# Layer 0 of a four-layer attention kernel: TensorE and VectorE in source order, an earlier normalisation, a look-up in three steps

## The chip, the cores and the metric

The kernel runs on one core of a Trainium2 chip. The metric is the device time of one execution in microseconds (us). A core has five engines that run side by side and wait for each other through semaphores: TensorE (PE; PEld is its loading of weights), VectorE (DVE), ScalarE (ACT), GpSimd (POOL) and SyncE (SP), which here issues the DMAs. Matrix products land in PSUM, the accumulator memory, and have to be evicted from there by VectorE or ScalarE before the same buffer can be used again.

## The reference

The input is four images of 56 x 56 positions with 256 channels in float32. Four layers follow one another; each adds its result to its input, and each normalises its input first over groups of eight channels. Only layer 0 matters here. It is attention over a 7 x 7 neighbourhood with zero padding, with eight heads of 32 channels:

```python
q = x @ wq.T + bq ; k = x @ wk.T + bk ; v = x @ wv.T + bv      # x: normalised
k_unf, v_unf = _unfold(k), _unfold(v)                          # 49 shifted copies, zero padded
logits = jnp.einsum('ndhw,ndkhw->nkhw', q, k_unf) * scale
attn = jax.nn.softmax(logits, axis=1)                          # over the 49 places
out = jnp.einsum('nkhw,ndkhw->ndhw', attn, v_unf)
return out @ wo.T + bo                                         # added to the layer's input
```

Layer 3 is attention in shifted windows with a bias that is read from a table of 169 rows by index: `bias = rel_bias_table[rel_index]`. The kernel makes that bias, with the window masks, while layer 0 runs.

## The kernel before, in words

Layer 0 works on two grids. The projections run over **chunks** of 448 positions (8 image rows), seven to an image (`NCH`), 28 in all. The attention runs over **blocks** of seven image rows, eight to an image (`NB0`), 32 in all, and each block has four **units** (`NTC`), pieces of 16, 12, 12 and 16 columns. Units 0 and 3 are the edge units, 1 and 2 the inner ones.

A chunk has seven steps. `prepare(r)` normalises the chunk on VectorE (L939, two instructions of 128x448), copies a few leftover columns and issues the load of the chunk after the next. `project_rows(r)` gives six steps: `values(0)`, `values(1)` (products L971, eviction with bias on VectorE L975, then a store of the values to DRAM), `keys(0)`, `keys(1)` (L945, four evictions on ScalarE L1190) and `queries(0)`, `queries(1)` (L945, evictions on ScalarE L1199). All of them, the output projection, the statistics and the look-up draw their PSUM tile from `ps_m`, which has two buffers in this layer.

`attend_pairs` runs the units. For unit w it does `logits(w)`: 16 products of float32 into the two tiles `ps_s` (L1058), a mask add on VectorE (`e`, L1065) followed by an exponential on ScalarE (L1066) for one half, and an exponential (L1068) followed by a product with a mask on GpSimd (L1069) for the other. Then come two adds on GpSimd for the unit before (`b`, L1078), then `w["fill"]()`, a list of steps of other work, then `products` of the unit before (L1087, into `ps_o`), and then its `done`, called `finish`: on VectorE a sum for blocks and units at the image's border (L1234), a reciprocal (L1237 or L1232) and the product that writes `attn` (L1239). `gather`, the first act of a unit, fetches the values it needs from DRAM.

`project_out(r)` is the output projection of block r in two steps (L945 with `w_wo`): each adds the residual on VectorE (`xr`, L1263); the second also takes the next layer's statistics (`bn_stats`, L894) and stores. `first_look(i)` takes the statistics of the next image's chunks (L894 on `x`), which `load(i, looks, "xs")` has fetched before. When all parts of an image are there, `group_stats` puts three steps on a list: `channels`, `mean` (a small product L912 and three small VectorE instructions on `dv`, L915 to L917) and `scale` (a second small product L921, then L922 and a power on GpSimd, L923). `step_stats` runs one of them; `known(l, b)` runs all that are pending.

`table_steps` makes the bias table of layer 3: seven calls of `look_up(q0)` and four of `mask(ty)`. One look-up casts indices and compares them with row numbers on VectorE (L1940, L1943), multiplies the resulting one-hot matrix with the table (L1947), copies the result (L1950), transposes it on TensorE (L1953) and copies again (L1954).

`stream` deals these steps out to the blocks, and `spread` cuts the list of a block into four equal parts. In layer 0 no engine is fixed, so this list is not the order of execution: a planner orders the instructions of each engine by what it expects to be ready and may move a step past others. Layer 1 has TensorE and VectorE in source order, layer 2 none, layer 3 four engines.

Of the kernel before, what the change touches and what calls it, by code (L numbers as in the profile page):

```python
# [24 lines left out]
FP = mybir.dt.float32  # L25
# [6 lines left out]
NIMG = 4  # L32
S = 56
T = S * S
C = 256
P = 128
CC = C // P
HD = 32
NH = 8
SCALE = HD ** -0.5  # L40
NCH = 7
CH = T // NCH
# [5 lines left out]
WN = 49  # L48
# [11 lines left out]
TR = 7  # L60
NB0 = S // TR
BT = TR * S
COLS = (0, 16, 28, 40, 56)
NTC = 4
# [766 lines left out]
def direct_blocks(ctx: ExitStack, tc: tile.TileContext, d: dict, watch):  # L831
# [44 lines left out]
    def ps_m():  # L876
        return psum_tile("m", m_bufs)
# [226 lines left out]
        products(held)  # L1104
        held["done"]()

    def spread(units, steps):

        n = len(units)
        for i, w in enumerate(units):  # L1110
            mine = steps[i * len(steps) // n:(i + 1) * len(steps) // n]
            w["fill"] = lambda mine=mine: [f() for f in mine]
            yield w

    def lazily(make, i, n):

        made = []
        return [lambda k=k: (made or made.extend(make(i)), made[k]()) for k in range(n)]
# [7 lines left out]
    def layer0(early, big, pool, brief):  # L1126
        types, width = tile_types()
        xs, looks = {}, {}
# [6 lines left out]
        def first_look(r):  # L1135

            add_stats(0, *divmod(r, NCH), looks.pop(r))
# [22 lines left out]
        def prepare(r):  # L1160
            c = r % NCH
            xn = xns[r] = brief.tile([P, CC, CH + P // 2], FP, tag="xn", name="xn0")
            x = xs.pop(r)
            at = left(c, CH)
            for h in range(CC):
                normalise(xn[:, h, at:at + CH], x[:, h, :], known(0, r // NCH), h)
            if at:
                end = left(c - 1, CH) + CH
                nc.scalar.copy(xn[:, :, :at], ahead[0][:, :, end - at:end])
            ahead[:] = [xn]  # L1170
            if 3 < r + 2 < NIMG * NCH:
                load(r + 2)

        def project_rows(r):

            b, g = divmod(r, NCH)
            xn = xns.pop(r)
            at = left(g, CH)
            v = brief.tile([P, 4, C], FP, tag="v", name="v0", bufs=1)

            def values(a):
                value_tiles(v, a, g, CH, xn, wv, bv0, vd[b])

            def keys(m):
                pm = project(wk, m * P, lambda h: xn[:, h, at:at + CH], CH)
                rows = pm.rearrange("p (r c) -> p r c", c=S)
                for i in range(NTC):
                    c0, n = key_range(*COLS[i:i + 2])
                    dst = (kE if i in (0, NTC - 1) else kI)[:, m, i // 2, 8 * g:8 * (g + 1), :]
                    nc.scalar.activation(dst, rows[:, :, c0:c0 + n], AF.Identity, bias=bk0[:, m:m + 1])  # L1190

            def queries(m):
                pm = project(wq, m * P, lambda h: xn[:, h, at:at + CH], CH)
                y = 8 * g
                while y < 8 * (g + 1):
                    i, y1 = y // TR, min((y // TR + 1) * TR, 8 * (g + 1))
                    if (b, i) not in q:
                        q[b, i] = brief.tile([P, CC, BT], FP, tag="q", name="q0", bufs=6)
                    nc.scalar.activation(q[b, i][:, m, (y - TR * i) * S:(y1 - TR * i) * S],  # L1199
                                         pm[:, (y - 8 * g) * S:(y1 - 8 * g) * S],  # L1200
                                         AF.Identity, bias=qbias[:, 0, m:m + 1], scale=SCALE)
                    y = y1

            return [lambda f=f, m=m: f(m) for f in (values, keys, queries) for m in range(2)]

        def pair(r, t):

# [59 lines left out]
            return [lambda m=m: step(m) for m in range(CC)]  # L1267

        def stream():
            n = NIMG * NCH  # L1270
            rows = []
            for c in range(2, n):
                rows += lazily(project_rows, c, 6)
                rows.append(lambda c=c: prepare(c + 1) if c + 1 < n else None)
            look_at = {}
            for b in range(NIMG - 1):
                for i in range(NCH):
                    look_at.setdefault(NB0 * b + min(i // 2 + (b == 0), 3), []).append((b + 1) * NCH + i)
            gone = 0
            for r in range(NIMG * NB0):  # L1280
                b, g = divmod(r, NB0)
                to = min(len(rows), (7 * (7 * r + 12)) // 8)
                steps, gone = rows[gone:to], to
                steps += [lambda i=i: first_look(i) for i in sorted(looks)]
                steps.append(lambda r=r: [load(i, looks, "xs") for i in look_at.get(r + 1, [])])
                for i in range(3 if g > 3 or g == 0 else 0):
                    steps.insert(2 * i, step_stats)
                if r:
                    steps += table[:3]
                    if len(table) in (1, 2, 3):  # L1290
                        steps.append(tables.close)
                    del table[:3]
                    at = (len(steps) + 1) // 2
                    steps[at:at] = project_out(r - 1)
                attns[r] = pool.tile([P, CC, BT], FP, tag="attn", name="attn0")
                yield from spread([pair(r, t) for t in range(NTC)], steps)

        for r in range(3):
            prepare(r)
            if r == 0:  # L1300
                load(3)
            if r < 2:
                for step in project_rows(r):
                    step()
        check_sizes(pool)
        tables = ExitStack()
        both = [tables.enter_context(tc.tile_pool(name=f"t{n}", bufs=n, side="right", reuse_waits="tile")) for n in (1, 2)]
# [613 lines left out]
    def table_steps(big, pool):  # L1921


        NR, NQ = 169, 7
        idx = big.tile([P, WN, WN], I32, name="idx")
        nc.sync.dma_start(out=idx.rearrange("p a b -> p (a b)"), in_=d["relidx"].to_broadcast([P, WN * WN]))
        row = big.tile([P, 2], I32, name="row")
        nc.gpsimd.iota(row, pattern=[[P, 2]], base=0, channel_multiplier=1)
        rowf = big.tile([P, 2], FP, name="rowf")
        nc.vector.tensor_copy(rowf, row)  # L1930
        tab = big.tile([P, 2, NH], FP, name="tab")
        nc.sync.dma_start(out=tab[:, 0], in_=d["table"][:P])
        nc.sync.dma_start(out=tab[:NR - P, 1], in_=d["table"][P:])
        t3 = big.tile([98, 4, 98], FP, name="t3")
        nc.sync.dma_start(out=t3, in_=d["c_m3"])
        base = big.tile([98, NH, WN], FP, name="base")

        def look_up(q0):
            idxf = pool.tile([P, NQ, WN], FP, tag="idxf", name="idxf")
            nc.vector.tensor_copy(idxf, idx[:, q0:q0 + NQ, :])  # L1940
            hot = pool.tile([P, 2, NQ * WN], FP, tag="hot", name="hot")
            for a, n in ((0, P), (1, NR - P)):
                nc.vector.tensor_scalar(hot[:n, a, :], idxf[:n].rearrange("p q k -> p (q k)"),  # L1943
                                        rowf[:n, a:a + 1], None, ALU.is_equal)
            pb = ps_m()
            for a, n in ((0, P), (1, NR - P)):
                nc.tensor.matmul(pb[:NH, :NQ * WN], lhsT=tab[:n, a, :], rhs=hot[:n, a, :], start=(a == 0), stop=(a == 1))  # L1947
            tb = pool.tile([NH, NQ, 98], FP, tag="tb", name="tb")
            for w in range(2):
                nc.vector.tensor_copy(tb[:, :, w * WN:(w + 1) * WN], pb[:NH, :NQ * WN].rearrange("p (q k) -> p q k", k=WN))  # L1950
            pt = ps_m()
            for q in range(NQ):
                nc.tensor.transpose(pt[:98, q * NH:(q + 1) * NH], tb[:, q, :], ident[:NH, :NH])  # L1953
            nc.vector.tensor_copy(base[:, :, q0:q0 + NQ], pt[:98, :NQ * NH].rearrange("p (q h) -> p h q", h=NH))  # L1954

        def mask(ty):
            m = pool.tile([98, NH, 98], FP, tag="m3", name="m3")
            for w in range(2):
                sl = slice(w * WN, (w + 1) * WN)
                nc.vector.tensor_tensor(m[:, :, sl], base, t3[:, ty:ty + 1, sl].to_broadcast([98, NH, WN]), ALU.add)  # L1960
            mv = m.rearrange("p (q j) k -> p q j k", j=4)[:, :, 2:4]
            nc.scalar.activation(mv, mv, AF.Exp)
            for pair in [3] if ty % 2 else range(3):
                nc.sync.dma_start(out=m3d[:, ty // 2, :, pair, :], in_=m)

        return [lambda q=q: look_up(q) for q in range(0, WN, NQ)] + [lambda ty=ty: mask(ty) for ty in range(4)]

    def check_sizes(pool):

# [178 lines left out]
        return tc.tile_pool(name=f"d{l}" + ("e", "", "w", "l")[k], bufs=(2, 1, 2, 2)[k],  # L2148
                            side="right" if l % 2 else "left", reuse_waits="tile")

    run(0, lambda own: layer0(*own), None, range(4))
    with pool_of(2, 0) as early, ExitStack() as ends:
        late = ends.enter_context(pool_of(1, 3))
        held = {}
# [102 lines left out]
```

## Time and profile before

| | us |
|---|---|
| median of 3 runs | 3981.41 (3980.17 to 3990.82) |
| the profiled execution | 3979.57 |
| its span, first to last instruction | 3977.7 |
| TensorE busy in the span | 3816.3 |
| VectorE busy | 2367.7 |
| GpSimd busy | 1745.9 |
| ScalarE busy | 1378.9 |
| layer 0, first logits to last residual product | about 38 to 802 |

The times of single instructions come from the profiled execution. Its span is what the profile's views divide up; the execution took 1.9 us more than the span. Layer 0 is about the first fifth. A row of groups or of waits names the line, the engine, the tile written and the tiles read.

### The profile page before, as it was taken

Reading aid. Unit: us, or ns where it says so; the run is one execution under the profiler, and the core shown is the slowest. Engines: PE = TensorE matmul, PEld = TensorE weight load, DVE = VectorE, ACT = ScalarE, POOL = GpSimd, SP = SyncE. Lnnn points to the kernel's source line nnn. Section 1 sums busy time; section 2 is a strip of 40 time slices with the busy share of each in tenths; the row PEclk is TensorE's granted clock in tenths of the full one; section 3 lists DMA queues with packets and bytes.
Section 4 is the critical chain, followed back from the end, with each engine's and each line's share of the span. In section 5 each row is a group of like instructions: output and inputs, shape, how many; then the busy total and the mean of one; then the engine's idle time right before and its main releaser. Section 6 shows DMA issues by size and latency. Waiting matters only on the chain. (4 is left out here: it accounts for less than half of the span.)

```text
span 3977.7 us, 92350 instructions
## 1 busy us (share of the span) xinstructions
PE 3816.3 (96%) x38871; PEld 2712.4 (68%) x38871; DVE 2367.7 (60%) x4431; ACT 1378.9 (35%) x2927; POOL 1745.9 (44%) x1883
## 2 busy tenths in 40 slices
PE   6999999889999999999999999999999999899998
PEld 4566666567777677776777767776676676566665
DVE  6777777734345544445444553446788877666665
ACT  3454545422222222222222222222555555344443
POOL 2576767721123312233112331123777777555555
PEclk9899999989999999999999999999999999999999
DMA  7343333320000100001000000001344443444443
GB/s 265 100 137 121 117 114 110 98 104 1 24 19 24 40 5 16 20 25 35 6 24 15 25 24 10 10 10 55 113 125 128 127 119 108 154 122 129 131 126 97
DMA packets 268659, 301.84 MB, mean 76 GB/s; under 512 B 25926, under 2 KB 260584, under 8 KB 267752
## 3 DMA queue, kind: packets, MB, share of 16 engines
q1 hardware_dynamic: 267946, 295.76, 24.4%
q8 instruction: 308, 5.05, 0.6%
q14 instruction: 117, 0.96, 0.1%
q10 hardware_dynamic: 288, 0.08, 0.0%
HBM read 203.39 MB, written 92.37 MB: 74 GB/s over the span
## 5 line engine op out<-in xcount | busy, mean ns | idle before, releaser
L1441 DVE TENSOR_TENSOR acc<-acc,ps_v 128x257 f32<-128x257 f32 x1104 | 463.4, 423 | 718.8 <-PE ps_v L1519 690.7
L1519 PE MATMUL ps_v<-xw,e 128*128 128x257 f32 x2208 | 612.3, 382 | 1.2 <-DVE acc L1441 1.2
L1514 PE MATMUL ps_o<-xw,at 128*128 128x257 f32 x2208 | 609.1, 380 | 0.0
L1409 PE MATMUL ps_s<-xnT,xd 128*128 128x512 f32 (+3 forms) x1344 | 573.2, 549 | 3.9 <-DVE xnT L1387 3.9
L1519 PEld LDWEIGHTS ps_v<-xw,e 128*128 128x128 f32 x2208 | 413.4, 189 | 142.4 <-issue 82.3
L1503 ACT COPY at<-ps_t 128x512 f32<-128x512 f32 (+3 forms) x332 | 170.4, 513 | 969.8 <-PE ps_t L1500 969.4
L1078 POOL TENSOR_TENSOR b<-e 126x336 f32<-126x336 f32 (+5 forms) x512 | 499.6, 996 | 9.3 <-ACT e L1066 1.2
L1514 PEld LDWEIGHTS ps_o<-xw,at 128*128 128x128 f32 x2208 | 419.3, 190 | 59.9
L945 PE MATMUL ps_m<-xn,w_wqkv 128*128 128x392 f32 x1024 | 375.5, 500 | 3.6 <-DVE v L975 1.9
L1402 POOL TENSOR_SCALAR xd<-xnT,vec 128x128 f32<-128x128 f32 x192 | 116.8, 619 | 569.9 <-PE ps_s L1409 566.1
L1069 POOL TENSOR_TENSOR e<-e,m0t 126x672 f32<-126x672 f32 (+3 forms) x128 | 238.5, 1863 | 266.5 <-ACT e L1068 253.5
L1069 POOL TENSOR_TENSOR e<-e,bias 119x784 f32<-119x784 f32 (+5 forms) x128 | 244.0, 1906 | 182.5 <-ACT e L1068 181.2
L1409 PEld LDWEIGHTS ps_s<-xnT,xd 128*128 128x128 f32 x1344 | 226.1, 191 | 142.0 <-issue 126.7
L1412 ACT ACTIVATE e<-ps_s 128x512 f32<-128x512 f32 x336 | 185.3, 552 | 348.4 <-PE ps_s L1409 341.4
L990 ACT ACTIVATE no<-rs 128x168 f32<-128x168 f32 (+2 forms) x256 | 93.8, 367 | 592.8 <-DVE rs L1841 280.3
L1087 PEld LDWEIGHTS ps_o<-e,vp 124*32 124x32 f32 (+3 forms) x8192 | 179.0, 111 | 141.6 <-issue 90.5
L945 PEld LDWEIGHTS ps_m<-xn,w_wqkv 128*128 128x128 f32 x1024 | 187.4, 190 | 125.2 <-ACT pr L2097 17.4
L1087 PE MATMUL ps_o<-e,vp 124*32 124x112 f32 (+3 forms) x8192 | 242.7, 255 | 6.0 <-POOL e L1069 4.4
L1066 ACT ACTIVATE e<-e 126x672 f32<-126x672 f32 (+5 forms) x256 | 219.5, 857 | 21.3 <-DVE e L1065 8.4
L939 DVE TENSOR_SCALAR xn<-x,gst 128x28 f32<-128x28 f32 (+4 forms) x368 | 207.4, 616 | 32.3 <-PE ps_m L945 22.9
L1841 DVE RECIPROCAL rs<-ps_o 128x196 f32<-128x196 f32 (+2 forms) x128 | 176.1, 1375 | 84.8 <-PE ps_o L1087 84.3
L971 PE MATMUL ps_m<-w_wqkv,xn 128*128 128x256 f32 (+1 forms) x800 | 206.0, 396 | 9.4 <-DVE xr L1876 6.0
(196 smaller groups left out, 6206.2 us busy)
## 6 DMA issues: line engine op xcount, KB each, us to landing
x<-xr SPq DMA_DIRECT2D x64, 392.0 KB
x<-in_x SPq DMA_DIRECT2D x53, 448.0 KB
x<-x SPq DMA_DIRECT2D x60, 392.0 KB
xr<-x SPq DMA_DIRECT2D x60, 392.0 KB
vd<-v SPq DMA_DIRECT2D x72, 256.0 KB
xr<-in_x SPq DMA_DIRECT2D x32, 392.0 KB
xr<-x SPq DMA_DIRECT2D x28, 448.0 KB
x<-xr SPq DMA_DIRECT2D x28, 448.0 KB
```

The lines of the kernel that those rows point to most:

```text
L939: nc.vector.tensor_scalar(dst, src, gst[:, h, 0:1], gst[:, h, 1:2], ALU.subtract, ALU.mult)
L945: nc.tensor.matmul(pm[:, :n], lhsT=w[:, h, col:col + P], rhs=rhs(h), start=(h == 0), stop=(h == CC - 1))
L971: nc.tensor.matmul(pm[:k, j * C:(j + 1) * C], lhsT=xn[:, h, first:first + k], rhs=w[:, h, :], start=(h == 0), stop=(h == CC - 1))
L1066: nc.scalar.activation(ev, ev, AF.Exp)
L1069: nc.gpsimd.tensor_tensor(parts(ev), parts(ev), w["emask"], ALU.mult)
L1078: nc.gpsimd.tensor_tensor(w["b"][a][:nk, :, :2 * nq].rearrange("p h (i c) -> p h i c", i=2), ev[:, :, :, 0, :], ev[:, :, :, 1, :], ALU.add)
L1087: nc.tensor.matmul(w["o"](k, i)[j * HD:(j + 1) * HD], lhsT=ones[:nk, :HD] if k else v(j, u), rhs=w["b"][j // 2][:nk, j % 2, i * nq:(i + 1) ...
L1409: nc.tensor.matmul(s[:, :n], lhsT=xd[j][:, h, :], rhs=xnT[:, h, first * P:last * P], start=(h == 0), stop=(h == CC - 1))
L1412: nc.scalar.activation(e[:, :n], s[:, :n], AF.Exp, scale=5.0)
L1441: nc.vector.tensor_tensor(acc[:, i, :], acc[:, i, :], pv[:, :C + 1], ALU.add)
L1514: nc.tensor.matmul(out[j][:, :C + 1], lhsT=e[:, col(i)] if i == j else at[:, col(i)], rhs=xw[:, i, :], start=(i == j), stop=(i == NB - 1))
L1519: nc.tensor.matmul(pv[:, :C + 1], lhsT=e[:, col(i)], rhs=xw[:, j, :], start=True, stop=True)
```

## The change

Four things are changed, all in layer 0.

1. The last line of the diff fixes TensorE and VectorE to source order for the whole layer; ScalarE, GpSimd and SyncE are still ordered by the planner.
2. `stream` is rewritten in the form that layer 2 has: each unit gets its own list `work[u]`. Three chunks are projected before the first block instead of two, and `needed(r)` says how many chunk steps have to be done by the end of block r: an even share, or what the next block reads, if that is more. The steps of a chunk alternate: values 0, keys 0, values 1, queries 0, keys 1, queries 1. The two steps of the output projection stand last in units 2 and 3, statistics first in units 0, 2 and 3, a first look in units 0, 1 and 2.
3. `prepare(c + 1)` stands behind the second of the six projection steps of chunk c and no longer behind the sixth, that is, half a chunk ahead.
4. `look_up` is cut in three: `look_up` (cast and compare), `rows_of` (product with the table and copies), `turn` (transposes and copy). They stand in units 0, 1 and 2 of a block, so that a block holds one look-up.

```diff
-    def spread(units, steps):
-
-        n = len(units)
-        for i, w in enumerate(units):
-            mine = steps[i * len(steps) // n:(i + 1) * len(steps) // n]
-            w["fill"] = lambda mine=mine: [f() for f in mine]
-            yield w
...
-            return [lambda f=f, m=m: f(m) for f in (values, keys, queries) for m in range(2)]
+            return [lambda f=f, m=m: f(m) for f, m in ((values, 0), (keys, 0), (values, 1), (queries, 0), (keys, 1), (queries, 1))]
...
-            for c in range(2, n):
-                rows += lazily(project_rows, c, 6)
-                rows.append(lambda c=c: prepare(c + 1) if c + 1 < n else None)
+            for c in range(3, n):
+                steps = lazily(project_rows, c, 6)
+                steps.insert(2, lambda c=c: prepare(c + 1) if c + 1 < n else None)
+                rows += steps
...
+            def needed(r):
+
+                b, g = divmod(min(r + 1, nb - 1), NB0)
+                last = min(TR * (g + 1) + 3, S)
+                c = next(c for c in range(NCH) if c == NCH - 1 or (c + 1) * CH // P * P >= last * S)
+                return max(min(len(rows), len(rows) * (r + 1) // (nb - 1)), 7 * (b * NCH + c - 2))
+
             gone = 0
-            for r in range(NIMG * NB0):
+            for r in range(nb):
                 b, g = divmod(r, NB0)
-                to = min(len(rows), (7 * (7 * r + 12)) // 8)
-                steps, gone = rows[gone:to], to
-                steps += [lambda i=i: first_look(i) for i in sorted(looks)]
-                steps.append(lambda r=r: [load(i, looks, "xs") for i in look_at.get(r + 1, [])])
-                for i in range(3 if g > 3 or g == 0 else 0):
-                    steps.insert(2 * i, step_stats)
+                to = needed(r)
+                work = [rows[gone + (to - gone) * u // NTC:gone + (to - gone) * (u + 1) // NTC] for u in range(NTC)]
+                gone = to
+                for u, i in enumerate(sorted(looks)):
+                    work[u].append(lambda i=i: first_look(i))
+                work[3].append(lambda r=r: [load(i, looks, "xs") for i in look_at.get(r + 1, [])])
+                for u in (0, 2, 3) if g > 3 or g == 0 else ():
+                    work[u].insert(0, step_stats)
                 if r:
-                    steps += table[:3]
-                    if len(table) in (1, 2, 3):
-                        steps.append(tables.close)
-                    del table[:3]
-                    at = (len(steps) + 1) // 2
-                    steps[at:at] = project_out(r - 1)
+                    for u in range(3):
+                        if table:
+                            work[u].append(table.pop(0))
+                            if not table:
+                                work[u].append(tables.close)
+                    for u, step in zip((2, 3), project_out(r - 1)):
+                        work[u].append(step)
                 attns[r] = pool.tile([P, CC, BT], FP, tag="attn", name="attn0")
-                yield from spread([pair(r, t) for t in range(NTC)], steps)
+                for u in range(NTC):
+                    w = pair(r, u)
+                    w["fill"] = lambda steps=work[u]: [f() for f in steps]
+                    yield w
...
-            if r < 2:
-                for step in project_rows(r):
-                    step()
+            for step in project_rows(r):
+                step()
+        prepare(3)
...
+            held[q0] = hot
+
+        def rows_of(q0):
+            hot = held[q0]
             pb = ps_m()
...
+        def turn(q0):
+            tb = held.pop(q0)
             pt = ps_m()
...
-        return [lambda q=q: look_up(q) for q in range(0, WN, NQ)] + [lambda ty=ty: mask(ty) for ty in range(4)]
+        return [lambda f=f, q=q: f(q) for q in range(0, WN, NQ) for f in (look_up, rows_of, turn)] + [lambda ty=ty: mask(ty) for ty in range(4)]
...
-    run(0, lambda own: layer0(*own), None, range(4))
+    run(0, lambda own: layer0(*own), {E.PE, E.DVE}, range(4))
```

## The prediction

> **What bounds the kernel now.** I read the page first: the span, the row of busy time and the slices.
>
> ```profile
> span 3977.7 us, 92350 instructions
> ...
> PE 3816.3 (96%) x38871; PEld 2712.4 (68%) x38871; DVE 2367.7 (60%) x4431; ACT 1378.9 (35%) x2927; POOL 1745.9 (44%) x1883
> ...
> PE   6999999889999999999999999999999999899998
> DVE  6777777734345544445444553446788877666665
> ```
>
> TensorE is busy nearly everywhere, so only its idle time and its slow stretches can be won or lost. A slice is 99.4 us; layer 0 is the first eight, and there VectorE (DVE) stands at 7 tenths, not 4: the second engine is near its limit just where the change works. The changed program's instruction order, read engine by engine, differs from the old one only up to the end of layer 0; behind it the order is the same on all five. So I asked for the windows of the four images of layer 0 (the first from the first logits at 38 us, each cut where its block 7 stores its output) and for TensorE's waits in them. Columns: window and length, PE, PEld, DVE, ACT, POOL busy, granted clock, DMA share, GB/s.
>
> ```profile
> 38.00:258.20 220.20, 190.91 (x2742) 121.12 (x2741) 168.25 (x262) 91.72 (x214) 118.72 (x93) 0.91 0.53 156
> 258.20:439.50 181.30, 166.96 (x2846) 113.22 (x2844) 136.81 (x190) 91.17 (x216) 125.25 (x101) 0.99 0.38 115
> 439.50:620.70 181.20, 166.87 (x2845) 113.04 (x2844) 136.76 (x189) 91.13 (x216) 125.12 (x101) 0.99 0.38 116
> 620.70:802.00 181.30, 161.77 (x2958) 109.82 (x2956) 135.38 (x188) 86.31 (x198) 130.69 (x104) 0.94 0.33 102
> ```
>
> TensorE idles 29.3 us in the first, 14.3 in each middle one, 19.5 in the last: 77 us in all, plus what the low clock costs. The waits of the second image (what waited, for whom; us, times, longest):
>
> ```profile
> PE ps_m L945 <- DVE attn L1239: 4.5, 2, 3.6
> PE ps_s L1058 <- DVE e L1065: 2.9, 5, 0.9
> PE ps_m L945 <- DVE dv L922: 2.1, 1, 2.1
> PE ps_m L921 <- DVE dv L917: 1.8, 1, 1.8
> PE ps_m L971 <- DVE xr L1263: 1.5, 2, 1.0
> PE ps_m L945 <- ACT kE L1190: 1.0, 1, 1.0
> ```
>
> The last row matters most. It is one place, in the timeline: a unit whose filling is keys, queries, output projection, three products for two `ps_m` buffers.
>
> ```profile
> 334.03 1.12 PE L1058 MATMUL ps_s<-q,kI 32*126 32x84 f32 x32
> ...
> 336.56 0.85 DVE L1065 TENSOR_TENSOR e<-ps_s,m0t 126x672 f32<-126x672 f32 x1
> ...
> 337.44 0.76 ACT L1066 ACTIVATE e<-e 126x672 f32<-126x672 f32 x1
> ...
> 338.11 0.37 ACT L1190 ACTIVATE kE<-ps_m,vec 128x152 f32<-128x152 f32 x1
> ...
> 339.35 1.58 PE L945 MATMUL ps_m<-attn,w_wo 128*128 128x392 f32 x4 [0.99 <-ACT kE L1190]
> ```
>
> Mask add on DVE (after the previous finish), exponential on ACT, then the eviction of the keys, then the third product: it starts 5.3 us after the unit, 0.99 us late.
>
> [...] the key eviction above sat ready behind the exponential. [...] behind the 5.7 us wait at 60 us, four 448-column matmuls took 3.36 us instead of 1.67. [...] the normalise of 448 columns took 0.42 to 2.41 us, mean 1.03 in the second image, and the three `dv` ops of 128x2 up to 2 us each.
>
> **The change part by part.** The sum is made against the profiled execution: 3979.6 us, span 3977.7 plus 1.9 around it; the median shown, 3981.4, is 1.8 above it.
>
> *What goes.* (a) The output projection moves to units 2 and 3 of a block, the last `attn` of the block before is written in unit 0: the waits for attn vanish in images 0 to 2, 4.2 + 4.5 + 4.5 = 13. In the last image they sit in blocks without filling and at the drain, and stay. (b) The old order pulled the 42 bn_stats (0.61 us) of images 1 to 3, with their 21 loads, into the first 120 us, and ran up to three table look-ups in one unit. DVE was late with values (11.2 + 2.3 us of waits in image 0) and look-up copies (3.1): 16.6. The new order takes the statistics two or three tiles per block and one look-up per block. (c) Waits for `xr`, 0.9 + 1.5 + 1.5 = 4. (d) Clock: 0.91 over 191 busy us of image 0 is up to 17 us; I take 10, as short waits remain. Sum 44.
>
> *What comes.* The block of eight products (v, k, v, q, k, q and two o) is now v | k | v q o | k q o, where the old order mostly had two to a unit. (e) Third product after k and q: 15 units at the measured 1.0 = 15. (f) Third product after v and q: the v eviction queues on DVE behind the mask add, this behind the finish of an edge unit (0.39 + 1.55 + 0.39), this in unit 1 behind a pair of normalises (2.07 mean). From the start of the unit that is 3.6 + 0.9 + 0.7 = 5.2 us against 4.6 for the three groups ahead on PE (1.05 + 1.95 + 1.6); with bn_stats in the units before, up to 2 late. 10 units at 0.8 = 8. (g) Seven table blocks. Step one (cast 0.6, two compares 1.4) and two bn_stats (1.2) stand ahead of a finish, so the next mask add is some 2 us late and with it the evictions: four units q v T / v q T / k q T at about 1.9. With k t o and q t o the third product is up after 3.2 us and its buffer free at 5.3 and 5.0: three at 2.1, three at 1.8. Together 19. (h) Statistics: the early `prepare` of a new image calls `known`, which runs the pending steps at once: matmul, three `dv` ops, matmul, power on POOL, on an in-order PE. Three times; one chain is 1 us free and up to 4.5 with POOL in the way; the old order paid 3.9 as well, so I add 3 each. In blocks 20 and 28 the `dv` ops (3.5 to 4.1 in the trace) stand before a v eviction in a v q o unit: 2.5 each more. Together 14. (i) The even share against what the next block needs leaves blocks 18 and 22 nearly empty, 26 empty and 23 overfull: 6. Blocks 26, 30, 31 without filling replace the old 29 to 31, at 17.3 us a block either way: 0. Sum 62.
>
> *Costed at nothing.* Three chunks before the stream instead of two and a bit: the same matmuls, earlier. The x loads, v stores, gathers and residual loads keep their number on SP (one row more); xs has four slots, and a DMA share of 0.38 covers them; if a load came late, DVE would stand on its bn_stats with the mask add behind, about 2 us a time. `prepare` earlier: covered by the half chunk of matmuls (5 us). POOL keeps its order.
>
> Net: 62 - 44 = +18, so 3997.6 against the profile and 3999 against the median; I say **3998 us**.
>
> Bounds. Unseen are (f), (g), (h), (i) as such, each from neighbouring rows: 0 to 15, 9 to 28, 3 to 22, 1 to 10. A gain from any is excluded: each is a wait added. (e) lies between 8 (ACT free earlier) and 18. Savings: 30 to 55, by how much clock and bn_stats congestion really go. So the whole runs from 21 - 55 = -34 to 93 - 30 = +63; the ends together are unlikely.
>
> **Rivals.** *Main: two buffers, three products.* For it: the 0.99 us case, seen twice in the middle images. **R1, faster.** The waits at DVE and clock in images 0 to 2 are removed, and the ring is milder because each eviction is ready sooner than my serial count. For it: DVE is idle 44 us of 181 per image, and the first image is 39 us longer than the others. With savings 55 and costs 31 (e 12, g 9, h 6, rest 4): -24, 3957. It decides where a third product costs less than about 0.4 us on average. **R2, no change.** What VectorE loses in order it gains in evenness: costs 46, savings 44; 3983. **R3, much slower.** DVE becomes the bound of the first image: a block of mask adds 3.9, finishes 7.7, residuals 2.4, values 1.1, normalises 2.1, bn_stats 2.4, look-up 3.2 is 22.8 us of DVE against 22 to 23 of PE; at 27 us a block the seven table blocks cost 15 more: +35, 4016. **R4, it does not act**: excluded, the orders differ.
>
> **How the numbers follow.** About 0.3%, 12 us, is what a measurement can tell from no change. Main 0.42, of which 0.05 falls short of 12 us; R3 0.15; R2 0.13; R1 0.30. So slower 0.37 + 0.15 = 0.52, same 0.05 + 0.13 = 0.18, faster 0.30. The likeliest case alone spans 3990 to 4010. The range 3946 to 4030 takes in R1 and R3 with some 12 us on either side; beyond it I leave 1 to 2 in 10.
>
> **What would show it.** Right: waits of `ps_m` L945 for kE and q evictions rise from 1 us to about 5 us in the middle images, waits for attn fall to nothing there, bn_stats of x are spread over 500 us, image 0 is no shorter than before by over 10 us. Wrong: middle images under 181 us; a first image under 205; idle of TensorE in layer 0 under 70 us in all; the clock at 0.97 or more in the first 250 us.

## The result, and the profile after

The changed kernel takes 4025.09 us (median of 4 runs, 4020.46 to 4026.93) against 3981.80 for the kernel before, run beside it: 43 us slower, a ratio of 1.0104 with a 95% interval of 1.0092 to 1.0117. The direction is the one forecast and the time lies in the forecast's range, but the shift does not fit: +16 was forecast, +43 measured. The profiled execution took 4026.93 us with a span of 4025.1, 47.4 more than the span before.

The page of the changed kernel, the same rows as before:

```profile
span 4025.1 us, 92357 instructions
...
PE 3832.5 (95%) x38871; PEld 2716.4 (67%) x38871; DVE 2380.8 (59%) x4431; ACT 1377.3 (34%) x2927; POOL 1749.9 (43%) x1883
...
PE   7788989989999999999999999999999999899998
DVE  5778777753444544445434454445687877666665
```

TensorE issued the same 38,871 matmuls and was busy 16 us longer. VectorE's first eight slices are as full as before. The windows of the four images, cut at the same stores (the first logits now come at 48.85 us, since three chunks lie ahead of them instead of two; columns as before):

```profile
48.85:279.27 230.42, 191.83 (x2880) 122.61 (x2880) 168.37 (x228) 88.32 (x205) 124.90 (x97) 0.87 0.34 105
279.27:467.91 188.64, 166.89 (x2794) 111.14 (x2796) 146.72 (x211) 91.61 (x215) 129.63 (x102) 0.96 0.52 147
467.91:664.64 196.73, 173.76 (x2858) 115.28 (x2850) 142.99 (x206) 90.62 (x215) 125.53 (x100) 0.97 0.37 113
664.64:850.04 185.40, 163.79 (x2856) 109.40 (x2844) 132.03 (x185) 83.86 (x193) 123.67 (x98) 0.94 0.32 101
```

Layer 0 ends at 850.0 us instead of 801.5: 48.5 us later. All of the loss is here; what follows took 1.1 us less. The 48.5 us have two parts. Over the whole of layer 0, start included, TensorE's busy time rose from 708.6 to 727.2 us and its idle time from 92.9 to 122.8. So **29.9 us are more waiting and 18.6 us are the same products at a lower clock**: the first image fell from 0.91 to 0.87, the two middle ones from 0.99 to 0.96 and 0.97. The clock records of the two traces agree: in layer 0 the clock was halved for 68 us before and for 113 us after. (Image by image the lengths don't compare, as the new list moves products between images.)

The waits of TensorE in the second image, which answer to the six rows shown of before. The change moves some lines of the kernel: the evictions of keys (L1190 before) are now L1182, those of queries (L1199) L1191, the residual (L1263) L1255.

```profile
PE ps_s L1058 <- DVE e L1065: 9.4, 8, 1.6
PE ps_m L945 <- ACT q L1191: 3.4, 3, 2.5
PE ps_m L921 <- DVE dv L917: 3.3, 1, 3.3
PE ps_o L1087 <- POOL b L1078: 2.4, 4, 1.0
PE ps_m L945 <- ACT kE L1182: 1.6, 2, 1.0
PE ps_m L912 <- DVE mv L908: 1.2, 1, 1.2
```

The row of attn (4.5) is gone. The evictions of keys and queries cost 5.0 instead of 1.0, and the logits wait 9.4 us for the mask add where it was 2.9. In the first image the greatest rows are these:

```profile
PE ps_m L921 <- DVE dv L917: 8.3, 1, 8.3
PE ps_m L1960 <- ACT q L1191: 7.4, 2, 4.6
PE ps_m L1960 <- DVE v L975: 5.9, 1, 5.9
PE ps_s L1058 <- DVE e L1065: 4.5, 5, 1.1
PE ps_m L1960 <- ACT kE L1182: 4.4, 1, 4.4
```

L1960 is the product with the table, `rows_of` (L1947 before): 17.7 us of waiting in four places, not for its own operand but for a free `ps_m` buffer. Before, the look-up had one row in this image:

```profile
PE ps_m L1953 <- DVE tb L1950: 3.1, 4, 1.1
```

One of the four in the timeline, from the first unit of a block into its second (start, length, engine, line, operation):

```profile
125.08 2.28 DVE L939 TENSOR_SCALAR xn<-x,gst 128x448 f32<-128x448 f32 x1
125.86 1.99 PE L971 MATMUL ps_m<-w_wv,xn 128*128 128x256 f32 x8
...
127.29 1.14 DVE L894 BATCH_NORM_STATS2 st<-x 128x6 f32<-128x448 f32 x2
127.69 1.67 PE L945 MATMUL ps_m<-xn,w_wq 128*128 128x448 f32 x4
128.35 0.32 DVE L1949 CAST idxf<-idx 128x343 f32<-128x343 int32 x1
128.71 2.79 DVE L1952 TENSOR_SCALAR hot<-idxf,rowf 128x343 f32<-128x343 f32 x2
...
131.43 0.37 DVE L1226 TENSOR_TENSOR rs<-ps_o,outside 128x224 f32<-128x224 f32 x1
131.83 1.55 DVE L1229 RECIPROCAL rs<-rs 128x224 f32<-128x224 f32 x1
...
133.73 0.85 DVE L1065 TENSOR_TENSOR e<-ps_s,m0t 126x672 f32<-126x672 f32 x1
...
134.49 0.68 DVE L975 TENSOR_TENSOR v<-ps_m,bc 128x512 f32<-128x512 f32 x1
...
135.23 2.55 PE L1960 MATMUL ps_m<-hot,tab 128*8 128x343 f32 x4 [5.87 <-DVE v L975]
...
142.05 3.35 PE L945 MATMUL ps_m<-xn,w_wk 128*128 128x448 f32 x4
```

The filling of the first unit of this block is all VectorE's (normalise, bn_stats, cast, compares: 6.5 us in the lines shown) and has no product, so TensorE is through with it at once and already makes values and queries of the second unit while VectorE is still comparing. Finish, mask add and eviction of the values follow in source order; the third product waits 5.87 us for that eviction. Behind the wait the clock is half (from 131.97 to 145.63 us in the clock record): the table product takes 2.55 us (1.41 where nothing waited, below) and the keys still take 3.35 instead of 1.67, seven microseconds later.

### The profile page after: what moved, and what is told of

It is laid out like the page before. It is cut to its first block, busy times and chain, and to the rows that moved or that the text cites. A ratio compares the mean times of both kernels' runs of the same rounds, so it can differ in the third digit from the quotient of the medians.

```text
span 4025.1 us, 92357 instructions
## 1 busy us (share of the span) xinstructions
PE 3832.5 (95%) x38871; PEld 2716.4 (67%) x38871; DVE 2380.8 (59%) x4431; ACT 1377.3 (34%) x2927; POOL 1749.9 (43%) x1883
## 5 line engine op out<-in xcount | busy, mean ns | idle before, releaser
L945 PEld LDWEIGHTS ps_m<-xn,w_wqkv 128*128 128x128 f32 x1024 | 188.0, 190 | 127.1 <-ACT pr L2113 17.1
L939 DVE TENSOR_SCALAR xn<-x,gst 128x28 f32<-128x28 f32 (+4 forms) x368 | 211.9, 629 | 18.8 <-ACT q L1801 5.9
L1019 POOL TENSOR_TENSOR e<-e,m3l 98x784 f32<-98x784 f32 x64 | 118.3, 1848 | 217.7 <-ACT e L1016 217.7
```

The costliest lines, as they stand in the source:

```text
L939: nc.vector.tensor_scalar(dst, src, gst[:, h, 0:1], gst[:, h, 1:2], ALU.subtract, ALU.mult)
L945: nc.tensor.matmul(pm[:, :n], lhsT=w[:, h, col:col + P], rhs=rhs(h), start=(h == 0), stop=(h == CC - 1))
```

## The experiments

"New list" is the dealing of the changed kernel, "old list" that of the kernel before. Times are medians of four or more runs; each ratio is to the kernel before, run beside it on the same chip. The versions were timed on several chips, on which the kernel before had medians of 3980 to 3984 us, so a difference of some 5 us between two versions decides nothing.

**Order alone, list alone.** First the new list without the fixed engines:

```diff
-    run(0, lambda own: layer0(*own), {E.PE, E.DVE}, range(4))
+    run(0, lambda own: layer0(*own), None, range(4))
```

> The changed kernel with no engine fixed in layer 0: the new lists of units, the table in three steps, the early normalise, but the planner's order again. Theory A (the fixed source order costs: VectorE's table compares and statistics stand ahead of the finish and the mask add because nothing may pass them, TensorE then waits over 3 us and falls to half its clock): the planner moves them, no wait of 4 us for an eviction is left in the first image, clock there 0.91 or more, time 3970 to 3995. Theory B (the dealing costs: three products to a unit for two ps_m buffers, blocks overfull and empty, in whatever order): 4005 to 4025, with the same crowded blocks.

Measured 3958.08, ratio 0.9942 (0.9926 to 0.9959). Theory B fell, and theory A fell short of the gain: the new list by itself makes the kernel 23 to 25 us faster. The longest wait for an eviction that is left in the first image is 3.7 us. (In the first image of the changed kernel each of the four waits over 3 us, of 4.65, 5.87, 8.26 and 4.43 us, came with half clock, which lasted 6.8, 13.7, 17.1 and 10.2 us. That is no limit for other places: in the kernel before, a wait of 3.05 us at 44 us was followed by keys at 1.77 us, full speed.) Then the old list with the fixed engines, the same line changed the other way in the kernel before:

> The kernel before with TensorE and VectorE fixed to source order in layer 0 and nothing else changed. Theory A: slower than before by 20 us or more, since this list holds three whole look-ups in a unit and the statistics of the next image in the first 120 us, and nothing may pass them now. Theory B: the old list deals about two products to a unit, so the middle images keep 181 to 184 us and the whole stays within 10 us of before.

Measured 4023.82, ratio 1.0103 (1.0086 to 1.0120). Fixing the order costs 42 us on the old list and 67 on the new one. In the old list three whole look-ups stand in a unit, each with its product right behind its compares, and nothing passes them: the table product waits for its compares seven times, 22.8 us in all, three times for over 6 us. The first of these reads, in TensorE's timeline,

```profile
90.38 2.55 PE L1947 MATMUL ps_m<-hot,tab 128*8 128x343 f32 x4 [6.12 <-DVE hot L1943]
```

Theory A, +20 or more, held; theory B, that the old list would stay within 10 us, fell.

**Which engine's order.** The changed kernel with `{E.PE}` or `{E.DVE}` in place of both:

> The changed kernel with TensorE alone in source order in layer 0; the planner orders VectorE too. Theory A1 (VectorE's fixed order is the cost: casts, compares, bn_stats and the statistics chain stand in source order ahead of finish and mask add): 3955 to 3985, near the 3958 of the version with no engine fixed. Theory A2 (TensorE's fixed order is the cost: a product whose buffer or operand is late holds up the products of attention behind it): 4010 to 4025, near the changed kernel. Both together: in between.

Measured 3963.22, ratio 0.9940 (0.9923 to 0.9956).

> The changed kernel with VectorE alone in source order in layer 0; the planner orders TensorE. Theory A1: 4005 to 4025. Theory A2: 3955 to 3985, since TensorE can take the products of attention ahead of a table product or a third product that has to wait.

Measured 4014.36, ratio 1.0066 (1.0050 to 1.0083). Theory A1 held in both: VectorE's fixed order makes nearly all of the loss; fixing TensorE besides adds about 11 us, and fixing TensorE alone adds 5, which is not clear of noise. What VectorE's freedom does can be seen in the same block as above, now with TensorE alone fixed:

```profile
110.06 1.76 DVE L1952 TENSOR_SCALAR hot<-idxf,rowf 128x343 f32<-128x343 f32 x2
...
129.10 1.99 PE L971 MATMUL ps_m<-w_wv,xn 128*128 128x256 f32 x8
129.91 0.39 DVE L1231 TENSOR_TENSOR attn<-ps_o,rs 128x224 f32<-128x224 f32 x1
130.22 0.85 DVE L1065 TENSOR_TENSOR e<-ps_s,m0t 126x672 f32<-126x672 f32 x1
130.93 1.67 PE L945 MATMUL ps_m<-xn,w_wq 128*128 128x448 f32 x4
131.13 0.69 DVE L975 TENSOR_TENSOR v<-ps_m,bc 128x512 f32<-128x512 f32 x1
132.52 1.42 PE L1960 MATMUL ps_m<-hot,tab 128*8 128x343 f32 x4
...
134.83 0.68 DVE L1952 TENSOR_SCALAR hot<-idxf,rowf 128x343 f32<-128x343 f32 x2
```

Values, queries, table: three products in the same order, and no wait. The normalise and the compares of this look-up were done at 110 to 117 us, units earlier, and those of the next fill the gaps behind, so that finish, mask add and eviction of the values come without a break.

**The look-up out of the way.** The table steps run between the projection steps of chunks 1 and 2:

```diff
             for step in project_rows(r):
                 step()
+                if r:
+                    for f in table[:3]:
+                        f()
+                    del table[:3]
...
```

> The changed kernel with the whole look-up (seven look-ups, four masks) run between the projection steps of chunks 1 and 2, ahead of the first block; the blocks hold none. Theory C (the table blocks of the first image trip the clock: compares late by collisions with GpSimd, then mask add, eviction and third product late): waits at the table product (17.7 us) and its copies (4 us) vanish from the blocks, the clock of the first image goes from 0.87 to 0.95 or more, the start grows by 5 to 15 us, net 15 to 28 us faster than the changed kernel: 3997 to 4010. Theory B (the ring of two with three products to a unit, in all four images): 0 to 10 us faster, 4015 to 4025, and the first image still shows waits of 3 us and a clock under 0.92.

Measured 4001.00, ratio 1.0048 (1.0031 to 1.0064): 24 us faster than the changed kernel, as theory C had it, though by other parts than expected. The first logits came at 94 us, 45 later and not 5 to 15, with 15 us more idle time of TensorE and a clock of 0.76 there; the first image's blocks took 172.5 us at a clock of 0.98 instead of 230.4 at 0.87. (How long the compares take beside GpSimd can be read in the changed kernel: the two during which no GpSimd instruction ran took 0.38 and 0.40 us, the other twelve 1.15 to 2.12.) The third image kept its length, 198 us. With the planner's order the same edit brings nothing:

> No engine fixed in layer 0 and, besides, the whole look-up ahead of the first block. Theory C (the look-up in the blocks costs beside the order): the last wait at the table product (3.7 us) goes, the clock of the first image rises above 0.955, another 5 to 15 us below the 3958 of the version with no engine fixed: 3943 to 3953. Theory A alone (the planner already hides the look-up): no gain, 3955 to 3968, as the start grows by what the blocks save.

Measured 3962.08, ratio 0.9942 (0.9926 to 0.9959), no faster than 3958: theory A alone, the planner had already hidden the look-up.

Running only the casts and compares ahead of the first block would have separated VectorE's lateness from the third product at one stroke (written down beforehand: 12 to 22 us faster, or under 6). It has no time: with the seven one-hot matrices kept, 2.7 KB per partition are left in SBUF where the look-up's other tiles need 14.2. The edits below take the question in steps.

**Two products to a unit.** Both engines fixed, the table in its place, only the dealing changed: five projection steps to a block, cut 2, 1, 1, 1. The normalise keeps its place but is no longer a step of its own, so that a chunk counts six steps. `upto[r]` is the even share, raised ahead of time for what later blocks need.

```diff
-                steps.insert(2, lambda c=c: prepare(c + 1) if c + 1 < n else None)
+                if c + 1 < n:
+                    steps[2] = lambda c=c, f=steps[2]: (prepare(c + 1), f())
...
-                to = needed(r)
-                work = [rows[gone + (to - gone) * u // NTC:gone + (to - gone) * (u + 1) // NTC] for u in range(NTC)]
+                to = upto[r]
+                sizes = {4: (1, 1, 1, 1), 5: (2, 1, 1, 1), 6: (2, 2, 1, 1)}.get(to - gone, (1, 1, 1, 0))
+                work = [rows[gone + sum(sizes[:u]):gone + sum(sizes[:u + 1])] for u in range(NTC)]
```

> The changed kernel, both engines fixed, with the projection steps dealt 5 to a block (a few 4 or 6) and cut 2, 1, 1, 1 to the units, so that with the output projection no unit outside the table blocks has more than two products and no block between 0 and 25 is empty or overfull. Theory B (the third product for two buffers and the uneven dealing, costed at 15 + 8 + 6 us in the forecast, are real): images 1 and 2 fall from 189 and 197 us to 181 or less, 20 to 30 us faster than the changed kernel, 3995 to 4005. Theory A (order, the first image): images 1 and 2 gain under 5 us each, the whole stays at 4013 to 4025.

Measured 3950.40, ratio 0.9910 (0.9894 to 0.9927): 75 us faster than the changed kernel, far more than either theory gave; the middle images fell to 181.3 and 175.6, as theory B had it. Counted in the lists, the changed kernel has 43 of 128 units with three or more products and 62 with one or none; this one has 7 and 33. Its windows:

```profile
48.85:250.19 201.34, 176.69 (x2884) 114.79 (x2884) 162.30 (x229) 88.06 (x205) 125.14 (x98) 0.97 0.39 120
250.19:431.50 181.31, 166.33 (x2803) 113.42 (x2804) 149.13 (x211) 92.19 (x218) 126.34 (x99) 0.95 0.54 154
431.50:607.05 175.55, 164.91 (x2859) 113.51 (x2851) 142.69 (x206) 90.50 (x216) 126.21 (x101) 0.98 0.42 127
607.05:771.74 164.69, 152.15 (x2844) 103.81 (x2832) 131.56 (x184) 83.10 (x191) 127.04 (x101) 0.97 0.36 112
```

The first image lost 29 us of 230, and the table product of the third look-up, the one shown above with its wait of 5.87 us, now reads, in TensorE's timeline, without a wait:

```profile
125.94 1.41 PE L1964 MATMUL ps_m<-hot,tab 128*8 128x343 f32 x4
```

**Price of a third product.** The even dealing kept, the cut turned round to 1, 1, 1, 2, so that unit 3, with its output projection, has three: 35 units instead of 7. Unit 0 is left with a single product, so that the units with one or none rise too, from 33 to 61; the price measured is that of the two together.

> The version with two products to a unit (3950), its even dealing by blocks kept, but the steps of a block cut 1, 1, 1, 2 instead of 2, 1, 1, 1, so that unit 3 has a third product in 28 blocks (35 units with three products, as against 7; the changed kernel has 43). Theory D (with VectorE in source order a third product costs 2 us, half of it clock; 75 us for 36 units): 28 x 2.1 = +59, about 4009. The forecast's price of 0.8 to 1.0 a unit: +25, about 3976. Theory E (it was the overfull and empty blocks, not the third product): within 6 us of 3950.

Measured 3982.01, ratio 1.0003 (0.9992 to 1.0014): 31.6 us for 28 units, 1.1 each. Theory D's 2.1 fell. In the two profiles, idle time of layer 0 grew by 21.5 us, 0.77 a unit, and TensorE's busy time by 15.7: as a wait the forecast's price of 0.8 to 1.0 stood, and the clock came on top. (These sum to 37; but this execution was the fastest of twelve and took 13 us less behind layer 0 than the other. By layer 0 alone, and by the ratios, a unit costs 1.3.)

The reverse is the new list's own dealing to blocks with a cut of 2 : 2 : 1 : 1 (14 units of three or more, 38 of one or none):

```diff
-                work = [rows[gone + (to - gone) * u // NTC:gone + (to - gone) * (u + 1) // NTC] for u in range(NTC)]
+                cut = [gone + -(-(to - gone) * n // 6) for n in (0, 2, 4, 5, 6)]
+                work = [rows[cut[u]:cut[u + 1]] for u in range(NTC)]
```

> The changed kernel with its dealing to blocks untouched (overfull and empty blocks stay), but the steps of a block cut 2 : 2 : 1 : 1 over its units instead of evenly, so that units 2 and 3, which also carry the output projection, get fewer: 14 units with three or more products instead of 43, 11 of them in the table blocks. Theory D: 29 x 2.1 = 61 us faster, 3955 to 3975, images 1 and 2 at 183 us or less. Theory C (the table blocks of the first image): 5 to 20 us faster, 4005 to 4020. Theory E (dealing by blocks): under 10 us faster.

Measured 3959.06, ratio 0.9946 (0.9929 to 0.9964): this edit takes 66 of the 75 us away. Overfull and empty blocks are still there, and seven more units of three, and together they cost the 9 us that are left; theory E is out. Theory D's sum of 61 came true although its price had not: at 1.1 to 1.3, 29 units would bring 32 to 38 us. So the price is not one number, and no run shows what makes up the rest of the 66.

**The third product in a table block.** Two to a unit, but `sizes` is 1, 2, 1, 1 in blocks 1 to 7: one step moves from unit 0, where the compares are, to unit 1, where the table product becomes the third.

> The version with two products to a unit (3950), with one step of each of the seven table blocks moved from unit 0 to unit 1, where it makes the table product the third. Theory C: the table product waits 3 to 6 us again in four or five blocks and the clock falls to half behind it: 30 to 45 us slower, 3980 to 3995. The forecast's price of 1.9 us for such a unit: +13, 3963. No cost of the third product there: within 5 us of 3950.

Measured 3980.07, ratio 1.0000 (0.9992 to 1.0009): 29.7 us for seven units, 4.2 each, three to four times the price in unit 3, and at the near edge of theory C. Idle time of layer 0 rose by 18.9 us and busy time by 11.0. Then the compares of these look-ups moved one unit earlier, to unit 3 of the block before:

```diff
-                    for u in range(3):
+                for u in (3,) if r == 0 else (1, 2, 3) if r < 7 else (1, 2) if r == 7 else (0, 1, 2):
...
```

> The version with the table product as third (3980), with cast and compares of each look-up moved from unit 0 of its block to unit 3 of the block before, one unit earlier; product and transposes stay in units 1 and 2, unit 1 keeps its three products. Theory G (the third product is dear there because VectorE's cast and compares, 4 to 6 us where GpSimd is busy, stand ahead of the finish, the mask add and so of the evictions that free the buffers): the waits at the table product fall from 22 us to under 10, most of the 30 us come back, 3952 to 3965. Theory H (the wait belongs to a unit of three after a unit of one, wherever the compares stand): 3973 to 3983.

Measured 3964.16, ratio 0.9952 (0.9935 to 0.9968): 16 of the 30 us come back, about half of it and just inside theory G; theory H fell. (In the trace of the changed kernel the cast and the two compares of a look-up add up to 3.2 to 5.0 us; 4 to 6 was the author's estimate.) The waits of the first image say why not all. At the table product 5.9 us are left of 24.6, but VectorE's lateness shows elsewhere: the logits' wait for the mask add was 2.2 us and is now

```profile
PE ps_s L1058 <- DVE e L1065: 12.6, 8, 3.2
...
PE ps_m L1964 <- ACT q L1191: 4.0, 2, 3.8
...
PE ps_m L1964 <- ACT kE L1182: 1.9, 1, 1.9
```

**Statistics.** Two to a unit, a pending statistics step at the head of every unit, and some first looks of image 1 a block earlier:

```diff
...
-                for u in (0, 2, 3) if g > 3 or g == 0 else ():
+                for u in range(NTC):
                     work[u].insert(0, step_stats)
```

> The version with two products to a unit (3950), with a pending statistics step at the head of every unit of every block and the first looks of image 1 one block earlier, so that the early normalise finds its statistics ready and runs no chain on the spot. Theory F (the forced chain costs its waits of 3.5, 4.8 and 4.8 us[...]): 15 to 28 us faster, 3922 to 3935. Rival (the forecast's 3 us each): 9 us faster, 3941. No gain if the chain waits on GpSimd wherever it stands.

Measured 3945.35, ratio 0.9912 (0.9890 to 0.9934); 5 us below 3950 by the medians, no difference by the ratios, and 1.3 us in layer 0 of the two profiles. Waits for `dv` fell from 15.0 us to 7.4. Theory F and the rival asked for more; no gain is what this comes nearest to. Before the edit, the values behind the three waits of 3.49, 4.75 and 4.76 us took 3.62, 3.95 and 3.78 us instead of 1.99, and the logits and queries that followed were at full speed again, 1.12 or 1.13 and 1.77 us; theory F's range was the author's estimate.

**Even list, planner's order.**

> The version with two products to a unit (3950) with no engine fixed in layer 0. If source order on VectorE costs by itself: 15 us or more faster, 3925 to 3938. If it costs only where the list holds three products to a unit: within 6 us of 3950.

Measured 3929.02, ratio 0.9870 (0.9854 to 0.9887): source order costs 21 us even here. In the two profiles that is all waiting: TensorE idles 21.4 us less in layer 0, and its busy time is 2.5 us longer. So list and order are not one cost:

| list | planner orders | TensorE and VectorE in source order |
|---|---|---|
| old | 3981 (before) | 4024 |
| new | 3958 | 4025 (after) |
| two to a unit | 3929 | 3950 |

An uneven list costs 29 us where the planner may repair it and 75 where it may not. With the statistics edit on top:

> The two best edits together: the even list with a statistics step at the head of every unit (3945), and no engine fixed in layer 0 (3929 with the old statistics). If the statistics chain is a cost of its own, 5 us below 3929: 3921 to 3926. If the planner already moves it out of the way: 3926 to 3932.

Measured 3924.50, ratio 0.9857 (0.9840 to 0.9873), the fastest of all and 1.4% below the kernel before. The gain of 4.5 us over 3929 lies within the intervals.

## Why the prediction was right or wrong

**Right in direction, wrong in one term.** Against the profile, the sum was 62 of costs less 34 of waits removed (a, b, c), less 10 of clock (d). Measured in layer 0: idle +29.9 against +28; clock +18.6 against -10. The failed step is **(d)**, "Clock: 0.91 over 191 busy us of image 0 ... I take 10". It looked at the slow stretches that would go with the old waits and put no clock on the waits that came, though the same text had noted products of 3.36 us instead of 1.67 behind a wait of 5.7 us. The runs give a rough price: where waits were added, each microsecond of idle time came with 0.5 to 0.7 of slower products (18.6 for 29.9 in the change, 11.0 for 18.9 with the table product third, 15.7 for 21.5 with unit 3 third, 15.4 for 29.1 with the order fixed on the old list). It is not a constant: between the two orders of the even list it was nothing. Put on the forecast's own net +28 of waits at 0.62, the sum would have been 45; but 0.62 is read from this very result, so that is no test of it.

That the waits came out at the forecast's sum is in part luck, as errors cancel. Term by term, in the profile of the changed kernel against before:

- (a) held: no wait for attn is left in images 0 to 2 (13.2 us before). In the last image, where they were to stay, they fell from 6.1 to 2.6.
- (b) held for the values in image 0 (13.5 to 1.3 as a wait of projections), but the congestion came back at the table product, which is (g).
- (c) held: the waits for `xr` fell from 3.9 to 0.3.
- (e) 15: waits for keys and queries in images 1 to 3 are 14.0 us, from 2.2: 12 more. Held within its bounds.
- (f) 8: waits for values in images 1 to 3 are 12.1, from none. Low by a third.
- (g) 19: the table product, its transposes and copies wait 22.0 us in the first image, where 3.1 were before: 18.9 more. The sum held, its parts did not: the four units with the table product as the third waited 4.4 us each and not 1.9, and for the six with transposes in the middle, priced at 11.7, all other projections of the image together waited 4.9 for a buffer. So the waits came long and few, and behind long ones the clock fell.
- (h) 14: waits in the statistics chain are about 19 us, where the rows of before have about 11: some 8 more. Halving them in the even list gained at most 5. High.
- (i) 6: the edit of the cut alone leaves some 9 us for it. Held. But a cost stands in no term: the logits' waits for the mask add are 19.1 us, from 9.5. They go with the number of units of one product or none: 12.6 us with 33 such units (two to a unit), 18.8 with 61 (unit 3 third). No run varied these alone.
- The list has 43 units with three or more products; (e), (f) and (g) count 35.

**The split that was not made.** The forecast priced list and order as one. In the table above the list alone is worth -23 and the order on it +67. What lets the planner hide a third product, an eviction on VectorE ahead of the compares (as in the block shown with TensorE alone fixed), is the freedom that the last line of the diff took away; only its effects on single waits were costed.

**The rivals.** R1 said 3957 for waits removed and cheap third products: that is the time of the new list under the planner (3958), not of the changed kernel. R3 named 4016, nearest to the result, but for a reason that the profile denies: VectorE was to be the bound of the first image. It is busy 168.4 of 230.4 us there. It is late in its order, not full. (R3's own sum, 18 and 15 more, is +33 and not +35.) R2 and R4 did not occur. Of the signs named, those for "right" all came: key and query waits of 5 us in the middle images, no attn waits, bn_stats of `x` spread from 5 to 545 us, a first image not shorter. None of those for "wrong" did. None of them asked about the clock of the middle images, which is where a sign would have helped.

**A trap in the view of VectorE's waits.** The groups of the changed kernel show VectorE idle far longer ahead of the residual:

```profile
L1255 DVE SCALAR_TENSOR_TENSOR xr<-ps_m,vec,xr 128x392 f32<-128x392 f32 x64 | 39.9, 623 | 118.8 <-PE ps_m L945 118.8
...
L1226 DVE TENSOR_TENSOR rs<-ps_o,outside 128x224 f32<-128x224 f32 (+1 forms) x80 | 29.6, 369 | 35.4 <-PE ps_o L1087 34.0 <-ACT e L1066 1.3
```

Before, the two stood at 26.3 and 76.5 us, and the finish of inner units (the reciprocal L1224, before L1232) at 32.5 instead of 10.5. The output projection is now the last product before the attention products, so VectorE waits for it and no longer for them. The three together rose from 135 to 165 us, in a layer that is 48.5 us longer: most of the 118.8 is the same idle time under another name, not a cost.

## What to carry to other kernels

Before fixing the order of an engine, make the list even in both engines' work unit by unit. What served here was as many products per unit as there are PSUM buffers, two, and products in the same unit as the work of the evicting engine, so that neither ran ahead of the other. Judge list and order apart, as each has a price that depends on the other. And where waits fall on TensorE, cost them with the clock behind them: here each microsecond that was added brought 0.5 to 0.7 more, and half clock went with how little of a stretch of 3.41 us TensorE had filled: it followed all 17 stretches under 42% and none of the 311 of 80% or more (next section).

## What the runs showed of the hardware that was not expected

Half clock came behind short waits too, where they stood close together. In a unit of the changed kernel with a single product:

```profile
545.54 0.39 PE L1087 MATMUL ps_o<-b,ones 124*32 124x112 f32 x4 [0.29 <-POOL b L1078]
546.63 0.58 PE L1087 MATMUL ps_o<-b,ones 124*32 124x112 f32 x12 [0.71 <-POOL b L1078]
548.67 2.01 PE L1058 MATMUL ps_s<-q,kI 32*126 32x84 f32 x32 [1.46 <-DVE e L1065]
550.61 3.36 PE L945 MATMUL ps_m<-xn,w_wq 128*128 128x448 f32 x4
```

Three waits of 2.46 us in sum, none over 1.46, and the logits take 2.01 us instead of 1.12, the queries 3.36 instead of 1.67. Between well filled units, a single wait of 3.16 us (at 598 us, for `dv`) was followed by logits at 1.12 and by queries at 1.77, full speed. The clock records show more: in each of the two traces, before and after, every change of clock lies a whole multiple of 3.413 us behind the one before it (in the changed kernel at 77.36, 84.19, 131.97 and 145.63 us, for instance), and carried back to the start of the span the series begins at 2.27 us in the changed kernel and at 1.65 us in the kernel before. Nor had TensorE to be idle for the whole of such a stretch. Cut into these stretches, the two places read (columns as above, the clock third from the end):

```profile
544.99:548.40 3.41, 1.22 (x26) 0.50 (x18) 3.34 (x6) 0.48 (x2) 3.33 (x4) 1.00 0.70 219
548.40:551.81 3.41, 3.14 (x34) 2.58 (x35) 3.34 (x6) 1.65 (x4) 1.61 (x2) 0.50 0.20 55
...
596.19:599.60 3.41, 1.55 (x6) 0.76 (x4) 3.34 (x5) 2.49 (x7) 3.17 (x3) 1.00 0.43 144
599.60:603.01 3.41, 2.11 (x67) 1.93 (x70) 1.96 (x6) 0.47 (x2) 2.87 (x5) 1.00 0.02 5
```

TensorE filled the first stretch to 36%, and the clock was half in the next. The wait of 3.16 us lay across the end of a stretch, at 599.60 us; the stretches on its two sides were 45 and 62% full, and the clock stayed at 1.00. In layer 0 of the two traces, from the first logits on, each of the 17 full-clock stretches under 42% was followed by half clock, and none of the 311 of 80% or more. Between 50 and 60% it was 5 of 12, so how full a stretch is does not settle it alone; no run here varied that by itself.

VectorE's cast of 128x343 took between 0.32 and 4.20 us (mean 0.38 before, 1.47 after), the longest while GpSimd worked: it began at 68.64 us and ended at 72.84, 0.2 us after three instructions of GpSimd that had run without a break since 68.37. In the version with two products to a unit its mean is still 1.09, and no table product there waited over 0.4 us: the long casts stay, and cost little where no table product is the third for two buffers. The normalise shows the same: in layer 0 of the kernel before, the 16 of 448 columns during which no GpSimd instruction ran took 0.42 to 0.51 us, the other 40 took 0.50 to 2.41. That GpSimd is the cause is argued from such places, not tested.
